# A four-layer vision hybrid on one core: where the mask's scatters stand, how late chunks are forced, and work moved between VectorE, GpSimd and ScalarE

## The chip, the cores and the metric

The kernel runs on one core of a Trainium2 chip, as one program. The metric is the device time of that program in microseconds. A profiled execution also gives the span, from the first recorded instruction to the last, and the TensorE clock that was granted, as a share of full speed. Engines are named TensorE (PE), VectorE (DVE), ScalarE (ACT), GpSimd (POOL) and SyncE (SP); PEld is TensorE's loading of weights.

## What is computed

The input `x` is 4 images of 32 x 32 positions with 256 channels, in float32. Four layers follow one another, image by image, with nothing shared between images except weights and one attention mask. The reference, cut to what matters here:

```python
# layer 0: conv, then a selective scan over the 1024 positions, 512 channels x 64 states
x = gelu(depthwise3x3(layernorm(src) @ w_in + b_in))
dt_raw, B, C = split(x @ w_x);  dt = softplus(dt_raw @ w_dt + dt_bias)
h = exp(dt*A)*h + (dt*x)*B;  y = sum_n h*C          # step by step over the positions
x = src + layernorm(y + x*D_skip) @ w_out + b_out
# layer 1: 1x1 conv, grouped 3x3 conv, 1x1 conv, residual
# layer 2: attention over 1024 positions, 8 heads, under a mask given by a list of edges
mask = zeros((N, N), bool).at[edge_index[0], edge_index[1]].set(True)
attn = softmax(where(mask, Q @ K.T / sqrt(32), -inf));  x = x + layernorm(ln(x) + (attn @ V) @ Wo + bo)
x = x + moe(ln(x))                                  # 8 experts of 256, best two of a position
# layer 3: a selective scan with 512 channels x 16 states, then 8 experts of 512, best two
x = x + scan3(ln(x));  out = x + moe(ln(x))
```

## The kernel before

**The stream of scans.** Each image has one scan of layer 0 and one of layer 3. A scan is cut into four chunks `d` of 128 channels, a chunk into units of 128 partitions x 1024 positions, where a partition is one channel with one state. A chunk of layer 0 has 64 units, a chunk of layer 3 has 16; with 4 images that is 1280 units in all. `SCANS` fixes their order: (layer, image) = (0,0), (0,1), (3,0), (0,2), (3,1), (0,3), (3,2), (3,3). `scans` (L340 to L477) issues a unit `k` as follows. `load` fetches the step sizes of unit k+4 by DMA into `dA` (5 buffers). `decay` makes exp(dt*A) of unit k+2 on ScalarE. `first` spreads the inputs of unit k+1 over the states on TensorE, into the PSUM tile `ps_rep` (2 buffers). VectorE multiplies `ps_rep` by the rows of B and runs the scan instruction into `h` (5 buffers); GpSimd multiplies `h` by the rows of C in place; and every second unit `pair` sums over the states of two units on TensorE into `ps_y`. So each unit takes two instructions of VectorE, one of ScalarE, one of GpSimd and some of TensorE, in a fixed order.

**The side work.** Everything else is written as generators that stop after every few instructions (`yield` with an estimated cost). `STAGES` lists them in order: `front(b)` of the four images (layer 0 up to the scan's inputs), `middle(b)` (`back0`, which ends layer 0 after its scan, layer 1, attention, the first mixture of experts, and `front3`, the inputs of layer 3's scan), and `last(b)` (the end of layer 3 and the second mixture of experts). A stage becomes available once the scan named beside it is done. `run` (L506) walks through the stream and, twice in each unit, lets the current stage go on by up to `TICKS` = 2 steps, as long as no engine's own clock of estimated work is ahead of VectorE's. The clocks are kept by the wrapper `Metered`, which adds an estimated cost for each instruction that goes through it (`Metered.COST`, L92 to L105; instructions issued through it carry L121 in the profile). `last(3)` is not in the list; `run` issues it when the stream is over.

**Forcing.** At unit k, `chunk(k + AHEAD)` with `AHEAD` = 12 (L461) fetches the inputs of a chunk if unit k+12 is a chunk's first. It calls `need(scan, d)` (L479), which lets the stages go on, with no unit in between, until the chunk's inputs (`parts`) are written. With every such step of a stage it also lets the work on the mask go on by `SORTS` = 2 steps, and at the end it sets all clocks to the furthest.

**The mask.** `mask_prepare` (L906) is one more generator, `mask_work`. It loads the list of edges, turns it into positions with transposes on TensorE, sorts each partition's positions in 68 steps on VectorE (L981 to L986), writes the sorted positions to `where`, and goes on into `scatter` (L992): 64 indirect DMAs, each of which writes one zero per partition to the mask in DRAM from GpSimd's queue, then four switches for longer lists that in this data leave their scatters out, and one DMA that casts the mask to bf16 (`maskT`). Outside `need`, `run` lets `mask_work` go on by one step in each unit.

**`steps`** (L538 to L598) ends `front` and `front3`. For each of 8 items of 128x512 it projects onto `ps_dt`, forms softplus from `sp_r`, `sp_e` and `sp_l` on ScalarE (relu, abs, exp, add 1, ln), VectorE (`add`, one instruction) and GpSimd (`add`, three instructions), and splits the product into three bf16 parts: a cast on ScalarE, the rest (`sp_x`) by a subtraction on VectorE, a second cast on ScalarE, and the lowest part on GpSimd. An item passes through `project`, `add`, `split`, `low` and `store` as through a pipe, one item apart.

**`attention`** (L1052) makes the scores `ps_sc`, their exponential `p`, and sums over keys with and without the values (`ps_at`), in `heads`. After every second pair of heads, four times an image, it takes the reciprocal of `sums` (128x512) on VectorE and multiplies `raw` by it on GpSimd (L1115 to L1120). `shift`, ahead of it, finds the number that is subtracted from the scores. The mixtures of experts work with `ps_h` (into an expert), `h_m` (gelu) and `ps_e` (out of it).

**`front`** (L634) loads its image `x` and the weights `w_in` first, then does the norm, the transposes, the projection and the 3x3 conv (`pad`, `ps_cv`), the projection to B, C and the step sizes, and `steps`.

Of the kernel before, what the change touches and what calls it, by code (L numbers as in the profile page):

```python
# [7 lines left out]
F32 = mybir.dt.float32  # L8
BF16 = mybir.dt.bfloat16
I32 = mybir.dt.int32  # L10
AF = mybir.ActivationFunctionType
ALU = mybir.AluOpType
# [4 lines left out]
P = 128  # L17
NB = 4
L = 1024
TB = L // P  # L20
C = 256
# [16 lines left out]
SAFE = 40.0  # L38
SORTS = 2
AHEAD = 12  # L40

# [82 lines left out]
class Hybrid:  # L126
    def __init__(self, ctx, tc, a, out):
        self.ctx, self.tc, self.nc, self.a = ctx, tc, tc.nc, a
        self.out = out.rearrange("b h w c -> (b h w) c")
        nc = self.nc  # L130
        self.const = const = ctx.enter_context(tc.tile_pool(name="const", bufs=1))
        self.dram = ctx.enter_context(tc.tile_pool(name="dram", bufs=1, space=DRAM))

        self.ident = const.tile([P, P], F32, name="ident")
        make_identity(nc, self.ident)
        self.identb = const.tile([P, P], BF16, name="identb")
        nc.vector.tensor_copy(self.identb, self.ident)

        order = const.tile([P, NEXP], I32, name="order")
        nc.gpsimd.iota(order, pattern=[[-1, NEXP]], base=NEXP, channel_multiplier=0)  # L140
        self.order = const.tile([P, NEXP], F32, name="orderf")
        nc.vector.tensor_copy(self.order, order)
        self.eps = {}
        for e in (1e-5, 1e-3):
            self.eps[e] = const.tile([P, 1], F32, name=f"eps{len(self.eps)}")
            nc.vector.memset(self.eps[e], e)

        self.mem = {}

# [190 lines left out]
    def scans(self, mp, psum):  # L340
# [9 lines left out]
        for scan in SCANS:  # L350
# [2 lines left out]
                (scan, d, c, i, j)  # L353
                for d in range(DC) for c in range(2) for i in range(32 // G) for j in range(2)
            ]
        chunks, rows = {}, {}
        state = {}
        y = None

        def chunk(k):  # L360

            if k >= len(units):
                return
            scan, d, c, i, j = units[k]
            if (c, i, j) != (0, 0, 0):
                return
            n = self.states[scan[0]]
            self.need(scan, d)
            if d == 0:
                bct = self.mem["bc", *scan]  # L370
                pair = []
                for t in range(2):
                    x = mp.tile([P, L], F32, tag=f"rows{t}", name=f"rows{t}", bufs=2)
                    for g in range(P // n):
                        nc.sync.dma_start(x[g * n : (g + 1) * n, :], bct[t * n : (t + 1) * n, :])
                    pair.append(x)
                rows[scan] = pair
            S = mp.tile([3 * 32, 4, L], BF16, tag="S", name="S", bufs=2)
            for s in range(3):
                nc.sync.dma_start(  # L380
                    S[32 * s : 32 * s + 32, :, :],
                    self.mem["parts", *scan, d][s].rearrange("(j p) t -> p j t", p=32),
                )
            chunks[scan, d] = S

        def load(k):
            if k >= len(units):
# [70 lines left out]
        decay(1)  # L458
        first(0)
        for k in range(len(units) + 4):  # L460
            chunk(k + AHEAD)  # L461
            load(k + 4)
            first(k + 1)
            decay(k + 2)
# [14 lines left out]
    def need(self, scan, d):  # L479

        late = False
        while ("parts", *scan, d) not in self.ready:
            if self.advance() is None:
                raise RuntimeError(f"{scan} waits for a stage that waits for it")
            late = True
            for _ in range(SORTS):
                next(self.mask_work, None)
        if late:

# [16 lines left out]
    def run(self):  # L506
# [4 lines left out]
        with tc.tile_pool(name="scan", bufs=1) as mp, tc.tile_pool(  # L511
            name="scps", bufs=1, space=PSUM
        ) as psum, tc.tile_pool(name="sdps", bufs=1, space=PSUM) as side, tc.manual_schedule():
            self.side_psum(side)
            self.mask_work = self.mask_prepare()
            clock = self.clock = dict.fromkeys(Metered.COST, 0.0)
            self.nc = Metered(nc, clock)
            for n, _ in enumerate(self.scans(mp, psum)):
# [19 lines left out]
    def steps(self, fp, key, w, src, chunks, bias, u):  # L538
# [33 lines left out]
        def split(item):  # L572
# [3 lines left out]
            X = fp.tile([P, 3, 512], BF16, tag="parts", name="parts", bufs=3)  # L576
            rest = tile2("x", 2)
            nc.scalar.copy(X[:, 0, :], x)
            nc.vector.tensor_tensor(rest, x, X[:, 0, :], ALU.subtract)
            nc.scalar.copy(X[:, 1, :], rest)  # L580
            got[item] = rest, X

# [51 lines left out]
    def front(self, b):  # L634
# [3 lines left out]
        with tc.tile_pool(name=f"f{b}", bufs=1, side="right") as op:  # L638
# [2 lines left out]
            nc.sync.dma_start(w_dt, self.a["L0_conv_w_dt"])  # L641
            u = op.tile([P, DC, L], F32, name="u0")
            with tc.tile_pool(name=f"fa{b}", bufs=1, side="right") as fp:
                x = fp.tile([P, TB, C], F32, name="x0")
                nc.sync.dma_start(x, self.image(self.a["x"].rearrange("b h w c -> (b h w) c"), b))
                w_in = self.weight(fp, "L0_conv_w_in", 2)
                pads = [fp.tile([P, 34, 34], F32, name=f"pad{i}") for i in range(2)]
                for i in range(2):
                    nc.gpsimd.memset(pads[i], 0.0)
# [256 lines left out]
    def mask_prepare(self):  # L906
# [16 lines left out]
        with tc.tile_pool(name="mprep", bufs=1) as mp:  # L923
# [5 lines left out]
            for a in range(2):  # L929
# [6 lines left out]
                    raw[:rest, full, :], edges[a, full * P * P :].rearrange("(r p) -> r p", p=P)  # L936
                )
                raws.append(raw)
            yield from [None] * 6
            for a, raw in enumerate(raws):  # L940
                rawf = mp.tile([P, full + 1, P], F32, tag="rawf", name="rawf", bufs=2)
                nc.vector.tensor_copy(rawf[:, :full, :], raw[:, :full, :])
# [44 lines left out]
            nc.vector.tensor_scalar(lin, order, 0.0, 2.0 * L * L, ALU.is_le, ALU.mult)  # L987
            nc.vector.scalar_tensor_tensor(lin, order, -1.0, lin, ALU.add, ALU.add)
            nc.vector.tensor_copy(self.where, lin)
        yield from self.scatter()  # L990

    def scatter(self):  # L992
# [35 lines left out]
    def prepare2(self, st, psum):  # L1028
# [17 lines left out]
        )  # L1046
        self.onesb = self.const.tile([P, P], BF16, name="onesb")
        nc.vector.memset(self.onesb, 1.0)
        self.ones = self.const.tile([P, 32], F32, name="ones32")
        nc.vector.memset(self.ones, 1.0)  # L1050

    def attention(self, b, tb):  # L1052
        nc, tc, vec = self.nc, self.tc, self.vec
        with tc.tile_pool(name=f"at{b}", bufs=1, side="right") as op:
# [48 lines left out]
            with tc.tile_pool(name=f"ac{b}", bufs=1, side="right") as fp:  # L1103
# [3 lines left out]
                for nh in range(2):  # L1107
# [3 lines left out]
                    for hp in range(4):  # L1111
                        yield from self.heads(fp, raw, sums, qT, kT, v, maskT, mT, nh, hp)
                        if hp % 2:
                            c = hp // 2
                            nc.vector.reciprocal(sums[:, c, :], sums[:, c, :])  # L1115
                            yield 2.0
                            nc.gpsimd.tensor_tensor(
                                raw[:, c, :], raw[:, c, :], sums[:, c, :], ALU.mult
                            )
# [614 lines left out]
```

## Time and profile before

The three timed runs of the kernel before took 6986.5, 7001.59 and 7013.21 us; the median is 7001.59 us. The profile is of one further execution:

| what | value |
|---|---|
| span of the profiled execution | 6998.6 us |
| its own time | 7000.6 us |
| instructions in the span | 66,229 |
| mean granted TensorE clock | 0.816 |
| GpSimd's `h` times rows, 1280 of them | 3029.4 us, 2369 ns each |
| VectorE's scans, 1280 | 2924.8 us, 2285 ns each |
| VectorE's `ps_rep` times rows, 1280 | 1553.1 us, 1213 ns each |
| ScalarE's exponentials of `dA`, 1280 | 1445.6 us, about 1146 ns each |
| ScalarE's table loads, 496 | 636.4 us, 1283 ns each |
| VectorE's two instructions of a unit together | 4477.9 us of its 5202.2 |
| data moved | 939 MB, 134 GB/s over the span |

The busy times of a page are sums over one execution, and an engine's share is of the whole span. Since the work comes in stretches with different limits (a head before the first scan, the stream, a stretch with no scan near the end, and a tail), such a share says little about any one of them. For that one reads the page's 40 slices, where VectorE falls to 2 tenths and 4 tenths from slice 33 on while TensorE goes on, and the timelines of single engines. "Idle before, releaser" is the idle time of that engine ahead of a group's instructions, and what ended most of it.

### The profile page before, as it was taken

How to read it: one execution, taken by the hardware profiler on the slowest of the kernel's cores; microseconds unless marked ns; L12 is line 12 of the kernel's file. 1: busy time of each engine (PE TensorE's matmuls, PEld its weight loads, DVE VectorE, ACT ScalarE, POOL GpSimd, SP SyncE). 2: the span in 40 equal slices, each digit the busy share in tenths (PEclk: the TensorE clock that was granted, in tenths of full speed). 3: DMA queues.
4: the chain of work that ended last, by engine and by line, in shares of the span. 5: the costliest groups of instructions: out<-in, count | busy, mean ns of one | idle time of the engine just before them, and what ended most of it. 6: DMA issues, size and time to landing. Idle time of an engine off the chain costs nothing. (4 is left out here: it accounts for less than half of the span.)

```text
span 6998.6 us, 66229 instructions
## 1 busy us (share of the span) xinstructions
PE 5362.1 (77%) x20433; PEld 2215.4 (32%) x20516; DVE 5202.2 (74%) x4476; ACT 3455.6 (49%) x4157; POOL 3646.1 (52%) x1801
## 2 busy tenths in 40 slices
PE   6267877578898557879779778898698677867979
PEld 2011211032242022224235332253254322523556
DVE  7379899887898986789889877898899830247511
ACT  2346666234577333447658434577386332244511
POOL 0667677565557755555756554556656530045300
PEclk8577867579898577889779778898699779877989
DMA  2356666654456565446656655456666630145421
GB/s 70 88 147 169 172 172 170 173 141 112 123 139 180 159 174 128 116 120 172 176 150 164 181 135 134 114 141 175 170 167 167 161 82 1 49 115 154 109 63 33
DMA packets 395050, 939.01 MB, mean 134 GB/s; under 512 B 83268, under 2 KB 165776, under 8 KB 393040
## 3 DMA queue, kind: packets, MB, share of 16 engines
q1 hardware_dynamic: 392512, 932.10, 49.6%
q8 instruction: 172, 2.82, 0.2%
q0 software_dynamic: 2128, 2.13, 0.2%
q14 instruction: 238, 1.95, 0.1%
HBM read 844.17 MB, written 93.95 MB: 134 GB/s over the span
## 5 line engine op out<-in xcount | busy, mean ns | idle before, releaser
L121 POOL TENSOR_TENSOR h<-h,rows 128x1024 f32<-128x1024 f32 x1280 | 3029.4, 2369 | 2048.6 <-DVE h L121 1661.0
L121 DVE TENSOR_TENSOR_SCAN h<-dA,ps_rep 128x1024 f32<-128x1024 f32 x1280 | 2924.8, 2285 | 214.1 <-issue 94.5
L121 DVE TENSOR_TENSOR ps_rep<-ps_rep,rows 128x1024 f32<-128x1024 f32 x1280 | 1553.1, 1213 | 330.9 <-PE ps_rep L121 310.6
L121 ACT ACTIVATE dA<-dA,A_L_conv_A_log 128x1024 f32<-128x1024 f32 x1024 | 1152.0, 1145 | 714.8 <-DMA dA<-dt 629.4
L121 PE MATMUL ps_rep<-S,spread_L_conv_A_log 96*128 96x512 bf16 x2048 | 759.1, 461 | 789.5 <-DVE h L121 730.6
L121 PE MATMUL ps_y<-h,collect_L_conv_A_log 128*32 128x512 f32 x4096 | 758.7, 754 | 87.9 <-POOL h L121 87.7
L121 ACT ACT_TABLE_LOAD x496 | 636.4, 1283 | 72.3 <-PE ps_h L121 50.3
L121 PEld LDWEIGHTS <-spread_L_conv_A_log 96*128 96x128 bf16 x2048 | 163.7, 103 | 1552.1 <-DVE h L121 1213.9
L121 PE MATMUL ps_h<-xTm,we 128*128 128x512 f32 x1280 | 605.7, 609 | 6.9 <-ACT h_m L121 5.8
L121 PE MATMUL ps_e<-we,h_m 128*128 128x256 f32 x2560 | 589.5, 382 | 8.3 <-ACT h_m L121 8.3
L121 ACT ACTIVATE p<-ps_sc 128x512 f32<-128x512 f32 x512 | 277.9, 594 | 588.7 <-PE ps_sc L121 431.7
L121 ACT ACTIVATE dA<-dA,A_L_attn_A_log 128x1024 f32<-128x1024 f32 x256 | 293.6, 1148 | 475.5 <-DMA dA<-dt 440.7
L121 PEld LDWEIGHTS ps_e<-we,h_m 128*128 128x128 f32 x2560 | 483.1, 190 | 138.8 <-issue 46.0
L121 PE MATMUL ps_at<-p,v 128*32 128x512 f32 x1024 | 361.6, 622 | 65.8 <-ACT p L121 58.0
L121 PE MATMUL ps_rep<-S,spread_L_attn_A_log 96*128 96x512 bf16 x512 | 191.7, 465 | 265.2 <-DVE h L121 219.5
L121 ACT ACTIVATE h_m<-ps_h,cols 128x512 f32<-128x512 f32 x320 | 216.7, 687 | 301.1 <-PE ps_h L121 298.3
L121 DVE SCALAR_TENSOR_TENSOR tb<-ps_e,cw,tb 128x256 f32<-128x256 f32 x448 | 192.7, 473 | 200.4 <-PE ps_e L121 200.4
L121 PEld LDWEIGHTS ps_h<-xTm,we 128*128 128x128 f32 x1280 | 242.3, 193 | 287.9 <-issue 239.7
L121 PE MATMUL ps_sc<-qT,kT 32*128 32x512 f32 x1024 | 299.5, 660 | 0.0
L121 PE MATMUL ps_at<-p,ones 128*32 128x512 f32 x1024 | 277.6, 622 | 0.0
L121 PE MATMUL ps_cv<-pad,diag 128*128 128x512 f32 x576 | 260.0, 593 | 0.0
L121 PEld LDWEIGHTS ps_y<-h,collect_L_conv_A_log 128*32 128x32 f32 x4096 | 99.2, 119 | 457.7 <-issue 226.4
(361 smaller groups left out, 5429.6 us busy)
## 6 DMA issues: line engine op xcount, KB each, us to landing
dA<-dt SPq DMA_DIRECT2D x2048, 256.0 KB
dA<-dt SPq DMA_DIRECT2D x2048, 64.0 KB
we<-in_L_ffn_W_dram SPq DMA_DIRECT2D x64, 512.0 KB
parts<-parts SPq DMA_DIRECT2D x64, 384.0 KB
S<-parts SPq DMA_DIRECT2D x96, 256.0 KB
dt<-sp_r SPq DMA_DIRECT2D x64, 256.0 KB
y<-yo SPq DMA_DIRECT2D x128, 128.0 KB
y_back<-y SPq DMA_DIRECT2D x64, 256.0 KB
```

Of the source, the lines that this page charges most:

```text
L121: return got(*args, **kw)
```

## The change

Nothing of what is computed changes; only where and when some of it is done.

- **Head.** The first image `x0` and the weights `w_in0` get tiles of their own for the whole program and are loaded ahead of everything else; `front(0)` reads that `x0`, and every `front` reads that `w_in0`. The wait between the loading of the edges and their conversion grows from 6 to 24 steps of `mask_work`.
- **Scatters.** When the sort is over, `mask_prepare` sets `self.sorted` and yields. From then on `need` no longer lets `mask_work` go on, so that the scatters come one a unit from `run`.
- **Late chunks.** `chunks_ahead` replaces `chunk(k + AHEAD)`. A chunk's first unit is put on a list at 12 units ahead. It is fetched at once if its inputs are there; otherwise it waits on the list until they are or until it is `LATEST` = 5 units ahead, and only then is it forced through `need`.
- **`rest`.** The subtraction that makes `sp_x` in `split` goes from VectorE to GpSimd, as a fifth instruction of GpSimd for each item.
- **Reciprocals.** VectorE's reciprocal of `sums` goes. In its place ScalarE takes ln and exp(-ln) into a new tile `inv`, with a table preload ahead; GpSimd multiplies `sums` and `raw` by it; ScalarE forms 2 minus the product, and GpSimd multiplies `raw` by that (one Newton step). A constant tile `two` is added, and the steps of the generator there have other costs.

```diff
--- before.py
+++ after.py
@@ -38,6 +38,7 @@
 SAFE = 40.0
 SORTS = 2
 AHEAD = 12
+LATEST = 5
 
 
 
@@ -144,6 +145,10 @@
         for e in (1e-5, 1e-3):
             self.eps[e] = const.tile([P, 1], F32, name=f"eps{len(self.eps)}")
             nc.vector.memset(self.eps[e], e)
+
+        self.x0 = const.tile([P, TB, C], F32, name="x0")
+        nc.sync.dma_start(self.x0, self.image(a["x"].rearrange("b h w c -> (b h w) c"), 0))
+        self.w_in0 = self.weight(const, "L0_conv_w_in", 2)
 
         self.mem = {}
 
@@ -353,7 +358,7 @@
                 (scan, d, c, i, j)
                 for d in range(DC) for c in range(2) for i in range(32 // G) for j in range(2)
             ]
-        chunks, rows = {}, {}
+        chunks, rows, waiting = {}, {}, []
         state = {}
         y = None
 
@@ -382,6 +387,16 @@
                     self.mem["parts", *scan, d][s].rearrange("(j p) t -> p j t", p=32),
                 )
             chunks[scan, d] = S
+
+        def chunks_ahead(k):
+
+            if k + AHEAD < len(units) and units[k + AHEAD][2:] == (0, 0, 0):
+                waiting.append(k + AHEAD)
+            while waiting:
+                scan, d = units[waiting[0]][:2]
+                if waiting[0] - k > LATEST and ("parts", *scan, d) not in self.ready:
+                    break
+                chunk(waiting.pop(0))
 
         def load(k):
             if k >= len(units):
@@ -458,7 +473,7 @@
         decay(1)
         first(0)
         for k in range(len(units) + 4):
-            chunk(k + AHEAD)
+            chunks_ahead(k)
             load(k + 4)
             first(k + 1)
             decay(k + 2)
@@ -483,7 +498,7 @@
             if self.advance() is None:
                 raise RuntimeError(f"{scan} waits for a stage that waits for it")
             late = True
-            for _ in range(SORTS):
+            for _ in range(0 if self.sorted else SORTS):
                 next(self.mask_work, None)
         if late:
 
@@ -512,7 +527,7 @@
             name="scps", bufs=1, space=PSUM
         ) as psum, tc.tile_pool(name="sdps", bufs=1, space=PSUM) as side, tc.manual_schedule():
             self.side_psum(side)
-            self.mask_work = self.mask_prepare()
+            self.mask_work, self.sorted = self.mask_prepare(), False
             clock = self.clock = dict.fromkeys(Metered.COST, 0.0)
             self.nc = Metered(nc, clock)
             for n, _ in enumerate(self.scans(mp, psum)):
@@ -576,7 +591,7 @@
             X = fp.tile([P, 3, 512], BF16, tag="parts", name="parts", bufs=3)
             rest = tile2("x", 2)
             nc.scalar.copy(X[:, 0, :], x)
-            nc.vector.tensor_tensor(rest, x, X[:, 0, :], ALU.subtract)
+            nc.gpsimd.tensor_tensor(rest, x, X[:, 0, :], ALU.subtract)
             nc.scalar.copy(X[:, 1, :], rest)
             got[item] = rest, X
 
@@ -641,9 +656,14 @@
             nc.sync.dma_start(w_dt, self.a["L0_conv_w_dt"])
             u = op.tile([P, DC, L], F32, name="u0")
             with tc.tile_pool(name=f"fa{b}", bufs=1, side="right") as fp:
-                x = fp.tile([P, TB, C], F32, name="x0")
-                nc.sync.dma_start(x, self.image(self.a["x"].rearrange("b h w c -> (b h w) c"), b))
-                w_in = self.weight(fp, "L0_conv_w_in", 2)
+                if b == 0:
+                    x = self.x0
+                else:
+                    x = fp.tile([P, TB, C], F32, name="x0")
+                    nc.sync.dma_start(
+                        x, self.image(self.a["x"].rearrange("b h w c -> (b h w) c"), b)
+                    )
+                w_in = self.w_in0
                 pads = [fp.tile([P, 34, 34], F32, name=f"pad{i}") for i in range(2)]
                 for i in range(2):
                     nc.gpsimd.memset(pads[i], 0.0)
@@ -936,7 +956,7 @@
                     raw[:rest, full, :], edges[a, full * P * P :].rearrange("(r p) -> r p", p=P)
                 )
                 raws.append(raw)
-            yield from [None] * 6
+            yield from [None] * 24
             for a, raw in enumerate(raws):
                 rawf = mp.tile([P, full + 1, P], F32, tag="rawf", name="rawf", bufs=2)
                 nc.vector.tensor_copy(rawf[:, :full, :], raw[:, :full, :])
@@ -987,6 +1007,8 @@
             nc.vector.tensor_scalar(lin, order, 0.0, 2.0 * L * L, ALU.is_le, ALU.mult)
             nc.vector.scalar_tensor_tensor(lin, order, -1.0, lin, ALU.add, ALU.add)
             nc.vector.tensor_copy(self.where, lin)
+        self.sorted = True
+        yield
         yield from self.scatter()
 
     def scatter(self):
@@ -1046,6 +1068,8 @@
         )
         self.onesb = self.const.tile([P, P], BF16, name="onesb")
         nc.vector.memset(self.onesb, 1.0)
+        self.two = self.const.tile([P, 1], F32, name="two")
+        nc.vector.memset(self.two, 2.0)
         self.ones = self.const.tile([P, 32], F32, name="ones32")
         nc.vector.memset(self.ones, 1.0)
 
@@ -1112,8 +1136,19 @@
                         yield from self.heads(fp, raw, sums, qT, kT, v, maskT, mT, nh, hp)
                         if hp % 2:
                             c = hp // 2
-                            nc.vector.reciprocal(sums[:, c, :], sums[:, c, :])
-                            yield 2.0
+
+                            r = fp.tile([P, 512], F32, tag="inv", name="inv", bufs=2)
+                            self.log_table()
+                            nc.scalar.activation(r, sums[:, c, :], AF.Ln)
+                            nc.scalar.activation(r, r, AF.Exp, scale=-1.0)
+                            yield 1.3
+                            nc.gpsimd.tensor_tensor(sums[:, c, :], sums[:, c, :], r, ALU.mult)
+                            nc.gpsimd.tensor_tensor(raw[:, c, :], raw[:, c, :], r, ALU.mult)
+                            yield 1.0
+                            nc.scalar.activation(
+                                sums[:, c, :], sums[:, c, :], AF.Identity, bias=self.two, scale=-1.0
+                            )
+                            yield 0.5
                             nc.gpsimd.tensor_tensor(
                                 raw[:, c, :], raw[:, c, :], sums[:, c, :], ALU.mult
                             )
```

## The prediction

> **What bounds the kernel now.** I read the page's engine lines first, then a table of busy time by stretch, then the timelines at the places where the stretches meet.
>
> ```profile
> PE 5362.1 (77%) x20433; PEld 2215.4 (32%) x20516; DVE 5202.2 (74%) x4476; ACT 3455.6 (49%) x4157; POOL 3646.1 (52%) x1801
> ```
>
> No engine is full over the span, so the limits are local. The stretches follow from VectorE's timeline, by counting its 1280 scans from 0 ("units"): the first starts at 279.9 us, unit 1203 at 5707.0, unit 1204 at 6224.1, and the last ends at 6582.5. In the table the columns after the stretch are its length and the busy us (count) of PE, PEld, DVE, ACT and POOL, then clock, DMA share and GB/s.
>
> ```profile
> 0.00:279.90 279.90, 122.55 (x286) 52.76 (x286) 146.20 (x333) 75.67 (x130) 68.67 (x70) 0.71 0.20 61
> 860.20:954.60 94.40, 57.28 (x144) 8.96 (x143) 84.47 (x57) 66.79 (x86) 85.71 (x50) 0.54 0.56 158
> 2310.60:2494.00 183.40, 100.99 (x310) 11.72 (x302) 173.83 (x102) 59.07 (x52) 120.01 (x52) 0.50 0.60 158
> 5709.30:6222.00 512.70, 424.65 (x1580) 182.47 (x1591) 75.50 (x181) 167.24 (x277) 45.74 (x36) 0.93 0.09 28
> 6222.00:6582.50 360.50, 261.81 (x965) 117.83 (x965) 292.16 (x235) 195.91 (x205) 207.07 (x101) 0.77 0.61 161
> 6582.50:6998.60 416.10, 371.42 (x1316) 251.60 (x1311) 58.47 (x150) 76.26 (x114) 17.07 (x13) 0.93 0.16 48
> ```
>
> Row 1 is the head, no scan. Row 3 is the bare stream, 51 units with no stage beside them: VectorE sets 3.60 us a unit. Row 2 is front(2)'s `steps`, 22 units at 4.29 us: VectorE and POOL are both near full. Row 4 is the hole: scan (3,3) waits for middle(3), PE works alone. Then scan (3,3) runs beside last(2), and the final row is the rest of last(2) and last(3), PE alone.
>
> In the head the timelines of VectorE and POOL show a queue, not work:
>
> ```profile
> 165.87 0.45 DVE L121 CAST where<-lin 128x544 int32<-128x544 f32 x1
> 175.08 0.69 DVE L121 SCALAR_TENSOR_TENSOR sp_e<-ps_dt,sp_e 128x512 f32<-128x512 f32 x1 [8.76 <-ACT sp_l L121]
> ```
> ```profile
> 234.25 0.97 POOL L121 DMA_INDIRECT mask_dram<-zero,where  x1 [1.43 <-DMA mask_dram<-zero,where]
> 236.65 0.97 POOL L121 DMA_INDIRECT mask_dram<-zero,where  x1 [1.43 <-DMA mask_dram<-zero,where]
> 237.64 1.27 POOL L121 TENSOR_TENSOR sp_l<-sp_l,sp_e 128x512 f32<-128x512 f32 x1
> ```
>
> `sp_e` was ready at 175.8, but 30 scatters at 2.40 us stand before `sp_l` on POOL until 237.6. In the stream a POOL burst reaches VectorE:
>
> ```profile
> 366.94 2.34 POOL L121 TENSOR_TENSOR h<-h,rows 128x1024 f32<-128x1024 f32 x1
> ```
> ```profile
> 372.27 1.23 DVE L121 TENSOR_TENSOR ps_rep<-ps_rep,rows 128x1024 f32<-128x1024 f32 x1 [6.82 <-PE ps_rep L121]
> ```
>
> Five instructions (361 to 367 us) hold this `h`, PE's `ps_y` behind it and the next `ps_rep`; VectorE stands 6.82 us.
>
> [...] here 128x512 takes 1.27 us on POOL and 0.68 on VectorE alone. [...] `sp_x` runs 0.682 to 2.294 us, median 1.513. [...] the trace's loads take 1283 ns, and one stands before each `steps` item. [...]
>
> **The change part by part.** The sum is made against the profiled execution: span 6998.6, its time 7000.6, 1.0 below the median of 7001.6. Positions are from the order of the changed program's instructions.
>
> *Head.* `x0` and `w_in` load first, the norm goes ahead of the sort, one scatter is left on POOL. PE's transposes still stand behind the edge transposes (about 58 us); the 97 us of conv and projection that before took 73.5 to 170 then end near 155. The sort now binds: 68 steps of 1.57 us (107) from about 57 end near 166. POOL starts `sp_l` at 168 instead of 237.6 (-70); from there to the first scan was 42.3, five rounds of about 8.5 us with two scatters each, and becomes about 40, as `rest` (1.29) takes their place. 279.9 becomes 208: -72. If the sort were hidden too, PE's chain would allow only 10 us more.
>
> *Scatters in the stream.* 63 of 64 now stand one behind each `h`: 2.37+1.03 = 3.40 us on POOL, under VectorE's 3.60, but nothing is left for `steps`: only two of its items fit in before unit 64, where 4 switches and the rest follow. Before, units 0 to 33 took 172.9 us. After, front(0) needs 74: 5 at 5, 59 at 3.75 (before, such units ran 3.6 with a few at 4 to 5), the last 10 with items, switches (27, as the gaps of 10.5 and 16.5 us at units 20 and 29) and the wait for front(1)'s x (15): 350. Less 41 bare units (148): +29. Without cover, at the 4.1 of the POOL-bound units, +50.
>
> *`rest` on POOL.* Off VectorE go 52 in the stream, about 1.5 us each. But POOL gets 5 instructions an item (6.35 us) at 3.60-2.37 = 1.23 us spare a unit, and the planner spaces an item 4.5 to 5 units instead of 3. So `steps` takes 35 to 37 units instead of 21 to 22. A unit then needs (4.75 x 2.37+6.35)/4.75 = 3.71 us of POOL and 3.74 of VectorE. The burst is longer than the slack before `h` is missed (about 5.5: three units less `h`, `ps_y`, `ps_rep`), and ScalarE's second cast, with the `dA` exponentials behind it, waits for POOL. I take 4.1 a unit (bounds 3.75 and 4.4). Before, 94.4+15 x 3.6 = 148; after 37 x 4.1 = 152; in the middles 96+50 = 146 against 35 x 4.1 = 144. Six such stages: +2 in all; bounds -75 and +65.
>
> *Reciprocals.* In heads stages a unit with one takes 9.7 us (units 584, 603, 618) instead of 3.6: 3.35 busy, 2.6 to 3.0 waiting for `sums`. Off the stream: 12 x 6.1 = 73. In their place stand a table load, Ln, Exp and a third pass on ScalarE (1.28+3 x 0.6) and two more POOL products (2.54); `dA` exponentials and the next `p` queue behind a pass that waits for POOL. No such wait is in the trace; bounds 0 and 6 us each, value 2.3. Net -45.
>
> *Late chunks.* LATEST acts at one place, (3,3): elsewhere the parts are ready 12 units ahead in both orders. But stretched stages push all later ones: middle(0) starts at unit 304 instead of 259, last(1) ends at 1173 instead of 1142, middle(3) starts at 1175 instead of 1155 and is forced at 1211 instead of 1204: 36 units of cover instead of 49. The stream gets 7 units (+25) and loses what stood in 1191 to 1204 (88 us, less 13 x 3.6: -41). Stream in all: 29+2-45+25-41 = -30.
>
> *Hole.* It takes 60 more `ps_sc` and 36 more `ps_at`: 9.5 rounds of 3.89 us (their period at 5714 to 5740): +37. The whole `shift` with its switch, +25 (estimate: 32 matmul pairs at 0.354 and four squares of 1.15, plus waits), and the mask's 2 MB load, +10. The reciprocal's chain was 3.35+1.27 and becomes 6.9 on three engines; with `p` behind it, +10 for four; POOL's `rest` in the last rounds, +6. +88.
>
> *After it.* 69 units instead of 76, but last(2) starts at 1229 instead of 1218: 18 units x 4.1, 30 as the 28 before (155.8+7), 21 x 4.25 = 328 against 358: -30. So 18 more `ps_h` (0.86) and 40 more `ps_e` (0.43) are left for the tail, by the chain's 6.87 us for 8 and 6.91 for 16: +33.
>
> Sum: -72-30+88-30+33 = -11. Span 6988, plus 2.0 around it, 6990.
>
> **Rivals.** *Even* (the forecast): the head's gain is paid out in the hole and the tail; 6990, own range 6967 to 7030. *POOL's bursts are hidden*: five `h` buffers absorb them, `steps` runs at 3.75 a unit (-75) and the reciprocal costs nothing in its new place (-28): 6890 to 6965, most likely 6930. For it: POOL is 52% busy, and before, bursts of four passed without a gap. Against: row 2 has POOL at 91%. *POOL becomes the bound* (slower): in `steps` each item's 6.35 us in one piece stops `h` and ScalarE's cast, so that VectorE stands 2 us or more an item beyond my value. At 4.4 a unit that is +65 and in units 0 to 74 +20: 7075. It decides from 4.25 a unit on; the gap of 6.82 us above is such a burst. *The change doesn't do what it says*: the later forcing covers nothing. By the order this is so already and is in the sum: 7 units are won, 20 lost before.
>
> **How the numbers follow.** Even 0.42, hidden 0.28, POOL bound 0.30. 0.5% (35 us) is about what a measurement of this kernel can tell from no change; the cases give faster 0.28, same 0.42, slower 0.30. The 8-in-10 range reaches into both neighbours: 6915 to 7075.
>
> **What would show it.** First scan near 208 us (200 to 220). Unit 74 some 350 us later. `steps` stages of 35 to 37 units at 4.1 us: under 3.85 speaks for hidden bursts, over 4.25 for POOL. No unit near 9.7 in the heads stages. A hole of about 605 us, PE full. A tail of about 449 after the last scan. A hole no longer than 517, or a first scan later than 240, would make the working wrong, not only a size.

## The result and the profile after

The changed kernel takes 7036.9 us (median of 8 runs, 7033.1 to 7040.3) against 7002.6 us for the kernel before (8 runs): a ratio of 1.0049, 95% interval 1.0038 to 1.0060. It is slower by half a per cent; 6990 was forecast, with a range of 6915 to 7075; the time lies inside it, on the wrong side of no change. The profiled execution has a span of 7035.0 us.

The engine lines of the changed kernel's page:

```profile
PE 5491.0 (78%) x20516; PEld 2227.5 (32%) x20516; DVE 5085.3 (72%) x4398; ACT 3466.5 (49%) x4196; POOL 3730.7 (53%) x1897
```

VectorE lost 117 us of work and GpSimd gained 85, as the change says. TensorE shows 129 us more with the same 20516 weight loads, which is the first sign of something else; "The clock" below comes back to it. The busy times by stretch, with the same columns as in the prediction; the rows are the head, the `steps` of `front(2)`, the hole, the units after it, and the tail:

```profile
0.00:207.90 207.90, 122.42 (x286) 54.33 (x286) 141.20 (x330) 71.37 (x126) 34.03 (x37) 0.81 0.25 82
977.00:1126.00 149.00, 89.62 (x245) 12.80 (x244) 132.60 (x86) 86.24 (x106) 136.67 (x80) 0.58 0.65 182
5646.00:6260.40 614.40, 491.01 (x1804) 207.92 (x1805) 63.47 (x183) 196.85 (x319) 63.83 (x51) 0.86 0.09 29
6260.40:6586.20 325.80, 225.20 (x806) 96.36 (x806) 260.31 (x208) 159.17 (x170) 193.92 (x97) 0.75 0.64 162
6586.20:7035.00 448.80, 403.73 (x1428) 269.96 (x1423) 62.72 (x160) 83.87 (x125) 17.06 (x13) 0.94 0.15 47
```

The head ends at 207.9 (forecast 208). `steps` has GpSimd 92% busy. The hole is 614.4 us long (605), the units after it take 325.8 (328) and the tail 448.8 (449). The stream from 207.9 to 5646.0 takes 5438 us where 5397 was forecast: the error sits there.

The head, in the timelines of VectorE and GpSimd:

```profile
169.69 0.44 DVE L122 CAST where<-lin 128x544 int32<-128x544 f32 x1
170.05 1.28 DVE L122 SCALAR_TENSOR_TENSOR sp_e<-ps_dt,sp_e 128x512 f32<-128x512 f32 x2
```
```profile
170.44 1.19 POOL L122 DMA_INDIRECT mask_dram<-zero,where  x1 [163.69 <-DVE where L122]
171.67 1.27 POOL L122 TENSOR_TENSOR sp_l<-sp_l,sp_e 128x512 f32<-128x512 f32 x1
```

`where` is done, one scatter goes, and `sp_l` follows at 171.7 instead of 237.6. In the stream the scatters stand between the products of GpSimd:

```profile
236.72 0.99 POOL L122 DMA_INDIRECT mask_dram<-zero,where  x1 [0.17 <-issue]
237.75 2.35 POOL L122 TENSOR_TENSOR h<-h,rows 128x1024 f32<-128x1024 f32 x1
240.41 1.00 POOL L122 DMA_INDIRECT mask_dram<-zero,where  x1 [0.31 <-DMA mask_dram<-zero,where]
```

The wait of 1.43 us that stood before each of them in the head is mostly gone here (0.17 us in the median of the stream's 63 scatters): it passes while the product runs (2.35 us).

Now the second reciprocal of image 0 (the chain of ScalarE, GpSimd, TensorE and VectorE, one view each, in the changed kernel):

```profile
1776.42 1.28 ACT L246 ACT_TABLE_LOAD   x1
1777.71 0.63 ACT L122 ACTIVATE inv<-sums 128x512 f32<-128x512 f32 x1
1778.37 0.63 ACT L122 ACTIVATE inv<-inv 128x512 f32<-128x512 f32 x1
```
```profile
1779.08 1.27 POOL L122 TENSOR_TENSOR sums<-sums,inv 128x512 f32<-128x512 f32 x1 [4.05 <-ACT inv L122]
1780.30 1.27 POOL L122 TENSOR_TENSOR raw<-raw,inv 128x512 f32<-128x512 f32 x1
1781.53 2.35 POOL L122 TENSOR_TENSOR h<-h,rows 128x1024 f32<-128x1024 f32 x1
1783.83 1.26 POOL L122 TENSOR_TENSOR raw<-raw,sums 128x512 f32<-128x512 f32 x1
```
```profile
1785.15 2.93 PE L122 MATMUL ps_wo<-w_L_attn_Wo,raw 128*128 128x256 f32 x6 [7.81 <-POOL raw L122]
```
```profile
1788.11 0.69 DVE L122 TENSOR_TENSOR y_at<-ps_wo,xa 128x512 f32<-128x512 f32 x1 [9.72 <-PE ps_wo L122]
```

and the same place in the kernel before, VectorE and TensorE:

```profile
1707.34 3.35 DVE L121 RECIPROCAL sums<-sums 128x512 f32<-128x512 f32 x1 [2.56 <-ACT sums L121]
1710.62 2.23 DVE L121 TENSOR_TENSOR_SCAN h<-dA,ps_rep 128x1024 f32<-128x1024 f32 x1
1715.06 0.69 DVE L121 TENSOR_TENSOR y_at<-ps_wo,xa 128x512 f32<-128x512 f32 x1 [2.22 <-PE ps_wo L121]
```
```profile
1712.10 6.33 PE L121 MATMUL ps_wo<-w_L_attn_Wo,raw 128*128 128x256 f32 x14 [4.78 <-POOL raw L121]
```

Read from the moment when `sums` is there (1707.3 before, 1776.4 after) to `y_at`: 7.7 us before, 11.7 after. GpSimd's four instructions are a queue in which an `h` of the stream (2.35) stands inside the chain. `ps_wo` waits 7.81 us for `raw` instead of 4.78, and TensorE makes its next `ps_rep` only behind it, at 1787.9. VectorE, which no longer has a reciprocal to do, waits at its own next instruction, `y_at`, which stands ahead of the next `ps_rep` product. Over the whole program, who waited before `ps_wo` and `y_at` (us, times), first before, then after:

```profile
  POOL raw L121: 76.3, 16
  PE ps_wo L121: 31.2, 16
```
```profile
  PE ps_wo L122: 384.9, 16
  POOL raw L122: 124.3, 16
```

The numbers for `raw` count each wait of TensorE twice, for the matmul and for its weight load. The numbers for `ps_wo` mix the stream with the hole, where VectorE has little else to do: 312.6 of the 384.9 us stand there. In the stream alone, at 12 of the 16 reciprocals, VectorE before waited 37.0 us for `sums`, worked 40.2 us on the reciprocals and waited 19.9 us at `y_at`, together 97 us; after, it waits 72.3 us at `y_at`. That alone would be a gain. The loss stands one instruction further on: in the three stages of `heads` beside the stream, VectorE's waits for the next `ps_rep` grew from 135 to 206 us.

Only every second reciprocal has a `ps_wo` behind it. Behind the first of each pair stand the next scores, and there the chain reaches TensorE through `p`. Three of ScalarE's instructions and one of VectorE's at the first reciprocal of image 0, in the changed kernel:

```profile
1699.14 1.28 ACT L246 ACT_TABLE_LOAD   x1
1703.10 0.72 ACT L122 ACTIVATE sums<-sums,two 128x512 f32<-128x512 f32 x1 [0.34 <-POOL sums L122]
1703.85 1.09 ACT L122 ACTIVATE p<-ps_sc 128x512 f32<-128x512 f32 x2
```
```profile
1717.28 1.23 DVE L122 TENSOR_TENSOR ps_rep<-ps_rep,rows 128x1024 f32<-128x1024 f32 x1 [10.09 <-PE ps_rep L122]
```

The scores are there at 1701.2, but `p` starts behind the table load, Ln, Exp, an exponential of `dA` and the third pass. TensorE waits for `p`, and VectorE then 10.09 us for its next `ps_rep`. The reciprocal's work went away from VectorE, and its waits became longer.

### The profile page after: what moved, and what is told of

The parts are those of the page before. It is cut to its first block, busy times and chain, and to the rows that moved or that the text cites. A ratio compares the mean times of both kernels' runs of the same rounds, so it can differ in the third digit from the quotient of the medians.

```text
span 7035.0 us, 66406 instructions
## 1 busy us (share of the span) xinstructions
PE 5491.0 (78%) x20516; PEld 2227.5 (32%) x20516; DVE 5085.3 (72%) x4398; ACT 3466.5 (49%) x4196; POOL 3730.7 (53%) x1897
## 3 DMA queue, kind: packets, MB, share of 16 engines
q8 instruction: 173, 2.83, 0.2%
## 5 line engine op out<-in xcount | busy, mean ns | idle before, releaser
L122 PE MATMUL ps_y<-h,collect_L_conv_A_log 128*32 128x512 f32 x4096 | 836.1, 749 | 134.3 <-POOL h L122 133.7
L122 PE MATMUL ps_at<-p,v 128*32 128x512 f32 x1024 | 397.1, 647 | 84.6 <-ACT p L122 72.4
L122 PEld LDWEIGHTS ps_h<-xTm,we 128*128 128x128 f32 x1280 | 243.1, 193 | 284.1 <-issue 235.4
L122 PEld LDWEIGHTS ps_y<-h,collect_L_conv_A_log 128*32 128x32 f32 x4096 | 116.5, 119 | 553.2 <-POOL h L122 320.8
L122 DVE TENSOR_TENSOR y_at<-ps_wo,xa 128x512 f32<-128x512 f32 x16 | 11.1, 692 | 384.9 <-PE ps_wo L122 384.9
```

The lines of the kernel that those rows point to most:

```text
L122: return got(*args, **kw)
```

## The experiments

Theory A: the new reciprocal is the larger loss, because its chain over three engines stands in TensorE's queue. Theory B: the rest on GpSimd costs little by itself, but the stages that it stretches take cover from the hole. Their rivals: GpSimd's load is the loss; the scatters in the stream give back what the head gains; late forcing brings or costs something of its own. Each run had the kernel before beside it, so the ratios to it are compared; 0.1% is 7 us.

| kernel | median us | ratio to before, 95% | head | stream | hole | units after | tail |
|---|---|---|---|---|---|---|---|
| before | 7002.6 | 1 | 279.9 | 5427 | 517 | 358 | 416 |
| changed | 7036.9 | 1.0049 (1.0038 to 1.0060) | 207.9 | 5438 | 614 | 326 | 449 |
| e1_recip_vector | 6947.9 | 0.9916 (0.9901 to 0.9930) | 207.5 | 5400 | 550 | 326 | 452 |
| e2_rest_vector | 7016.5 | 1.0019 (1.0012 to 1.0025) | 204.5 | 5538 | 513 | 329 | 433 |
| e3_both_vector | 6925.4 | 0.9883 (0.9868 to 0.9899) | 207.3 | 5473 | 486 | 328 | 433 |
| e4_latest12 | 7018.0 | 1.0019 (1.0012 to 1.0027) | 205.1 | 5413 | 607 | 359 | 433 |
| e6_no_newton | 6959.2 | 0.9948 (0.9934 to 0.9962) | 204.5 | 5480 | 505 | 332 | 433 |
| e7_newton_vector | 7029.2 | 1.0040 (1.0026 to 1.0053) | 204.5 | 5561 | 502 | 331 | 430 |
| e8_rest_unmetered | 6907.3 | 0.9861 (0.9846 to 0.9876) | 210.5 | 5447 | 488 | 325 | 444 |
| e9_both_latest12 | 6926.6 | 0.9890 (0.9875 to 0.9905) | 205.1 | 5430 | 518 | 358 | 420 |
| e10_both_scatter_head | 6961.8 | 0.9954 (0.9939 to 0.9969) | 235.4 | 5462 | 485 | 328 | 433 |
| e11_both_late_loads | 6904.8 | 0.9873 (0.9858 to 0.9888) | 209.8 | 5440 | 488 | 332 | 433 |
| e12_raw_vector | 6892.8 | 0.9847 (0.9834 to 0.9861) | 205.7 | 5439 | 484 | 319 | 443 |
| e13_best | 6897.1 | 0.9861 (0.9845 to 0.9878) | 207.7 | 5432 | 490 | 324 | 441 |

The stretches are of the profiled executions; the hole starts behind unit 1210, in e4, e9 and before behind 1203. A profiled execution can lie up to 18 us off its kernel's median: those of e1 (6937) and e10 (6944) are faster than their medians, that of e8 (6916) is slower.

**One part undone: the reciprocal, the rest, both.**

```diff
 # e1, e3 (the removed statements are shortened)
-r = fp.tile(...); self.log_table(); Ln; Exp(-1); sums *= r; raw *= r; sums = 2 - sums
+nc.vector.reciprocal(sums[:, c, :], sums[:, c, :])
+yield 2.0
 # e2, e3
-nc.gpsimd.tensor_tensor(rest, x, X[:, 0, :], ALU.subtract)
+nc.vector.tensor_tensor(rest, x, X[:, 0, :], ALU.subtract)
```

Expected of e1:

> The changed kernel with the reciprocal of the sums back on VectorE, all else as changed. Theory (the chain of the new reciprocal stands in TensorE's queue ahead of the next ps_rep and costs about 8 us more than VectorE's reciprocal at each of 12 places in the stream, and more in the hole): about 6960 us (6945 to 6980), 75 us below the changed kernel, with the heads stages at 325 to 340 us for 67 units as before the change. Rival (the rest on GpSimd is what makes the changed kernel slower, the reciprocal is neutral): 7025 to 7045.

Expected of e2:

> The changed kernel with the rest back on VectorE, the new reciprocal kept. Theory (reciprocal chain is the larger loss; the rest on GpSimd gains some 57 us in the stream and loses about 100 in the hole and the tail through 20 units less of cover): about 6980 us (6960 to 7000). Rival (the rest on GpSimd is the main loss): below 6950.

Expected of e3:

> The changed kernel with both the rest and the reciprocal back on VectorE: only the head, the scatters in the stream and the late chunks are left of the change. Theory: first scan at about 208 us instead of 280, units 0 to 74 as in the changed kernel, stages after that where they stood before the change, forced hole at unit 1210: about 6915 us (6900 to 6940). Rival (the scatters in the stream give back what the head gains): 6985 to 7005.

Undoing the reciprocal is worth 1.33% with the rest on GpSimd (changed to e1) and 1.36% with the rest on VectorE (e2 to e3): some 94 us, independent of the other part. Undoing the rest is worth 0.30% (changed to e2) and 0.33% (e1 to e3), some 22 us. So the reciprocal is the larger loss, as theory A has it, and e3 shows that the gain of the head stays when the scatters stand in the stream: -1.2%. e2 missed its forecast of 6980 by 36 us: the reciprocal costs 65 us in the stream and 27 in the hole (5538 against 5473, 513 against 486), more than was allowed for. The hole of e2 also holds two rounds of scores more than that of e3, some 8 of the 27 us.

Where in the stream: the three `heads` stages take 356.8, 368.0 and 365.2 us for 70 units in e2, and 324.1, 340.0 and 339.4 for 67 in e3. Less 9 bare units of 3.60 that is 54 us for 12 places, 4.5 each. Both kinds of place lose about the same: over eleven units, from two before the reciprocal on, the time beyond 3.60 us a unit has a median of 9.4 us at the six first places and 21.4 at the six second ones in e3, and of 14.0 and 26.1 in e2.

In the hole of e1 TensorE has 459.7 us of work against 491.0, and 90 us of gaps against 123:

```profile
5607.00:6157.00 550.00, 459.69 (x1696) 191.43 (x1711) 75.26 (x180) 176.05 (x294) 50.27 (x40) 0.90 0.08 27
```

The 31 us less of work are there in the main because three shorter `heads` stages let `middle(3)` begin at unit 1169 instead of 1175; the rest is the chain, four times, and a clock of 0.90 instead of 0.86.

**Which part of the reciprocal.** Both start from e2 (rest on VectorE). e6 leaves out the Newton step, so the reciprocal is only what ln and exp give:

```diff
 # e6
-nc.gpsimd.tensor_tensor(sums[:, c, :], sums[:, c, :], r, ALU.mult)
-nc.gpsimd.tensor_tensor(raw[:, c, :], raw[:, c, :], r, ALU.mult)
-nc.scalar.activation(sums[:, c, :], sums[:, c, :], AF.Identity, bias=self.two, scale=-1.0)
-nc.gpsimd.tensor_tensor(raw[:, c, :], raw[:, c, :], sums[:, c, :], ALU.mult)
+nc.gpsimd.tensor_tensor(raw[:, c, :], raw[:, c, :], r, ALU.mult)
 # e7
-nc.scalar.activation(sums[:, c, :], sums[:, c, :], AF.Identity, bias=self.two, scale=-1.0)
+nc.vector.tensor_scalar(sums[:, c, :], sums[:, c, :], -1.0, 2.0, ALU.mult, ALU.add)
```

Expected of e6:

> The kernel with the rest on VectorE and the new reciprocal, without its Newton step (two products of GpSimd and one pass of ScalarE less at each place, so the reciprocal is only as exact as ln and exp). The chain from sums to raw is then a table load, two passes and one product, 3.8 us by its rows, against 4.6 with VectorE's reciprocal. Theory (the length of the chain in TensorE's queue is the cost): most of the 91 us between this kernel with the Newton step (7016) and VectorE's reciprocal (6925) goes: 6940 (6925 to 6955). Rival (ScalarE's table load, Ln and Exp ahead of the exponentials are the cost): 6980 to 7005.

Expected of e7:

> The same with the Newton step kept, but its pass 2 - s on VectorE instead of ScalarE. Theory (length of the chain): little changes, and VectorE now waits for GpSimd's product: 7015 (7000 to 7035). Rival (the exponentials p and dA that queue on ScalarE behind the pass that waits for GpSimd are the cost): 6950 to 6985.

The waits before `ps_wo` and `y_at` in e6, then in e7:

```profile
  PE ps_wo L122: 278.3, 16
  POOL raw L122: 62.5, 16
```
```profile
  POOL raw L122: 154.6, 16
  PE ps_wo L122: 61.6, 16
```

TensorE has two waits to compare. In the three stages of `heads` beside the stream, each wait counted once (us):

| kernel | ratio to before | TensorE's wait for `raw` | for `p` |
|---|---|---|---|
| e3, VectorE's reciprocal | 0.9883 | 27 | 22 |
| e6, no Newton step | 0.9948 | 22 | 46 |
| e2, with Newton step | 1.0019 | 47 | 39 |
| e7, its pass on VectorE | 1.0040 | 62 | 23 |

Of the 1.36% between e3 and e2, 0.71% goes with the Newton step, and with it the longer wait for `raw`. e6 came out at 6959, between the forecast and the rival's range: 0.65%, 45 us, remain (28 us in the profiled executions, 20 of them in the hole), although TensorE waits less for `raw` than with VectorE's reciprocal. What remains longer is its wait for `p`, 46 us against 22, and what e6 still has on ScalarE ahead of `p` is a table load, Ln and Exp. No run takes these alone away, so the waits support this cause but do not isolate it. In e7 the wait for `p` is back at 23 us without the pass on ScalarE; but the pass now waits for GpSimd's product in VectorE's queue (59 us in these stages), `raw` comes later, and the whole is slower. So theory A, the length of the chain to `raw`, accounts for about half of the loss.

**The clock.** After a gap of TensorE its granted clock was also lower. Around the first reciprocal of image 0 (1701 us) the changed kernel's stretches read (the number after POOL's busy time is the granted clock), and TensorE's timeline ahead of them has the gap:

```profile
1704.50 1.55 PE L122 MATMUL ps_at<-p,v 128*32 128x512 f32 x2 [2.83 <-ACT p L122]
```

```profile
1702.00:1708.00 6.00, 3.50 (x12) 1.01 (x14) 5.00 (x3) 3.60 (x5) 6.00 (x5) 0.69 0.53 148
1708.00:1716.00 8.00, 7.74 (x24) 1.46 (x21) 0.00 (x0) 1.09 (x3) 4.44 (x2) 0.50 0.28 66
```

TensorE waits 2.83 us for `p`, then is busy for 7.74 of 8.00 us at a clock of 0.50, while VectorE does nothing (0.00). The kernel before has 1.00 at the same place (1628 to 1646 us). In the changed kernel's trace the granted clock is 0.5 or 1.0, 142 stretches of each, and each but the last, which runs past the end of the span, lasts 3.41 us or a multiple of it. In the 3.41 us from 1700.9 us on, which hold most of the gap, TensorE was 23% busy at a clock of 1.0; the next 13.65 us, four times 3.41, ran at 0.5, with TensorE over 90% busy in each of the four. Between 1000 and 3000 us of the changed kernel, 123 of the 124 pieces of 3.41 us that follow one with TensorE (matmuls and weight loads) less than half busy are at 0.5, and 323 of the 353 that follow one over 90% busy are at 1.0. From the first to the last scores of `heads` the mean clock went from 0.94 to 0.90 in image 0 (1564.7 to 1863.4 us before, 1620.1 to 1945.9 after) and from 0.93 to 0.90 in image 2 (4193.1 to 4500.5, 4189.3 to 4519.6); in image 1 it was 0.90 and 0.91 (2723.5 to 3037.6, 2679.6 to 3002.5). Over the whole span TensorE was busy at half clock for 1460 us instead of 1361, which is 99 of the 129 us by which its busy time grew, although the mean granted clock of the span, 0.822 against 0.816, did not fall. What the clock alone costs no run isolates.

**The rest on GpSimd, without the planner's count.** From e1, the instruction is issued past the wrapper that counts:

```diff
-nc.gpsimd.tensor_tensor(rest, x, X[:, 0, :], ALU.subtract)
+nc.what.gpsimd.tensor_tensor(rest, x, X[:, 0, :], ALU.subtract)
```

Expected of e8:

> The kernel with VectorE's reciprocal and the rest on GpSimd, where the planner is not told of the rest's cost on GpSimd, so that the steps stages take about 27 units instead of 37 and the middle of the last image starts at unit 1155 instead of 1169. Theory (the rest on GpSimd costs through the cover that the stretched stages take from the hole): below the 6948 us of the kernel in which it is counted: 6922 (6905 to 6938). Rival (GpSimd's bursts themselves cost): 6945 to 6975.

The same instructions on the same engine, 0.55% faster than e1. In the middles `steps` takes 27 units instead of about 37, at 4.4 us (118 us against 107 for 22 in the kernel before, so about 7 us less with 3.60 for each of the 5), and the hole is shorter:

```profile
5657.80:6145.50 487.70, 404.47 (x1450) 178.26 (x1461) 72.30 (x179) 156.42 (x258) 49.15 (x40) 0.90 0.09 29
```

55 us less of TensorE's work stands in it than in e1's, because `middle(3)` begins at unit 1155 again. The stream is 48 us longer, the hole 62 and the tail 8 shorter; the profiled executions differ by 22 us in all, the medians by 0.55%, some 38. Theory B holds: the price of the rest on GpSimd is the cover that the planner gives away for it, not GpSimd's bursts. Against the rest on VectorE (e3) it is 0.22% ahead, with intervals that overlap.

**LATEST.** `LATEST = 12` on the changed kernel (e4) and on e3 (e9):

Expected of e4:

> The changed kernel with LATEST = 12, so that late chunks are forced 12 units ahead as before the change. Theory: it acts in one place, scan (3,3); forced at unit 1203 instead of 1210, so 7 units' worth of stage work goes from the stream into the hole, about +15 us: 7052 (7040 to 7065). Rival (the later forcing brings nothing, or harms): 7020 to 7038.

Expected of e9:

> The kernel with the rest and the reciprocal on VectorE (6925 us) and LATEST = 12. Theory after the run with LATEST = 12 on the changed kernel: later forcing takes 7 units from the last stages beside scan (3,3), about 16 us of tail, and pays only if these units cover heavy TensorE work before the hole. Here heads runs in them (16 of 128 ps_sc pairs more), so both nearly balance: 6930 (6918 to 6945). Rival (later forcing never pays): 6900 to 6915.

e4 went against me: forcing 12 units ahead is 0.30% faster than 5, and its 7018.0 us lie even below the rival's range. The tail tells why: 433 us against 449. `last(2)` begins 18 units after the forced hole in both, so seven units later forcing are seven units less for its experts beside scan (3,3). And before the hole these seven units cover almost nothing (3.7 us each, the hole is 614 against 607 us). In e9, where the scores of `heads` run there, the hole grows from 486 to 518 when they are taken away, the tail shrinks by 13, and the times agree within their intervals.

**Scatters and early loads.** From e3, e10 lets the forcing go on with the scatters, and e11 loads `x` and `w_in` in each `front` as before:

```diff
 # e10
-for _ in range(0 if self.sorted else SORTS):
+for _ in range(SORTS):
 # e11
-self.x0 = const.tile([P, TB, C], F32, name="x0")
-nc.sync.dma_start(self.x0, self.image(a["x"].rearrange("b h w c -> (b h w) c"), 0))
-self.w_in0 = self.weight(const, "L0_conv_w_in", 2)
...
-w_in = self.w_in0
+w_in = self.weight(fp, "L0_conv_w_in", 2)
```

Expected of e10:

> The kernel with the rest and the reciprocal on VectorE (6925 us), where the forcing before the first scan goes on with the scatters after the sort as before the change, so that about 18 of the 63 go back into the head. Theory (a scatter in the head costs its 2.40 us in front of sp_l, and nothing measurable in the stream): first scan near 250 us, 6965 us in all (6950 to 6980). Rival (in the stream a scatter costs about the same): 6918 to 6935.

Expected of e11:

> The same kernel (6925 us), where x and w_in are loaded inside each front as before the change, after the loads of the setup. Theory (with the scatters gone from the head, the sort and the front's chain end within 10 us of each other, so that the early loads are worth little): first scan near 217 us, 6935 us in all (6925 to 6945). Rival (the early loads are the main gain of the head): above 6960.

In e10, 11 scatters stand before the first `sp_l` and 19 before the first scan:

```profile
192.50 0.97 POOL L122 DMA_INDIRECT mask_dram<-zero,where  x1 [1.46 <-DMA mask_dram<-zero,where]
193.48 1.29 POOL L122 TENSOR_TENSOR sp_l<-sp_l,sp_e 128x512 f32<-128x512 f32 x1
```

`sp_l` starts 22.0 us later (11 x 2.4 is 26), the first scan 28 us later, at 235.4 (near 250 was expected); the stream gets back 11 in the profiled executions. By the runs it is 0.71% slower, more than the trace explains; its five runs spread over 35 us, and the profiled one is the fastest of them. Either way, a scatter in the head costs more than in the stream. e11 has its first scan at 209.8 us instead of 207.3: the early loads bring the norm from 40.8 to 6.4 us, and nothing follows, because `where`, the sort's result, is written from 172.1 on instead of 169.5. Its median lies 20 us under the range that was expected, but its ratio and e3's overlap.

**Further.** e12 takes e8 and puts the last product on VectorE (`nc.vector.tensor_tensor(raw, raw, sums)`); e13 adds the late loads to e12.

Expected of e12:

> The kernel with the uncounted rest on GpSimd and VectorE's reciprocal (6907 us), where the product of raw with the reciprocal also goes to VectorE. Theory (what counts at these 16 places is how long ps_wo stands in TensorE's queue for raw): the chain is 0.6 us shorter and does not stand behind a product of GpSimd: 6895 (6885 to 6905). Rival (VectorE's own time is the limit there, 0.68 us more of it at each place): 6907 to 6920.

Expected of e13:

> What the runs so far point to, put together: the scatters in the stream, LATEST = 5, the rest on GpSimd but not counted by the planner, the reciprocal and the product of raw on VectorE, and x and w_in loaded inside each front. If the 20 us that the late loads gained without a change in the head are real, 6872 us (6865 to 6885); if they belonged to that chip and run, 6890 (6882 to 6900).

e12 is at 0.9847, 0.14% under e8, the size that was expected, but the intervals overlap. e13 is at 0.9861: the 20 us by which e11's median lay under e3's don't come again. e12 has the lowest ratio here, 1.5% under the kernel before (0.9834 to 0.9861) and 2.0% under the changed one; e8 and e13 cannot be told from it.

## Why the prediction was wrong

The sum of the prediction beside the profiled executions (us, after less before):

| step | forecast | measured |
|---|---|---|
| head | -72 | -72 |
| units 0 to 74 | +29 | +4 |
| `steps`, six stages | +2 | -56 |
| reciprocals in the stream | -45 | +51 |
| late chunks and the shifted start of `middle(3)` | -16 | -26 |
| stream, not priced | 0 | +38 |
| hole | +88 | +97 |
| units after it | -30 | -33 |
| tail | +33 | +33 |
| sum | -11 | +36 |

Inside the stream the measured column is the time of the units of a stage less 3.60 us for each, after less before; for the units 0 to 74 it is 324.4 - 172.9 - 41 x 3.6, and the late chunks have 7 units (25 us) added. That the sum missed by only 47 us is in part luck: the reciprocals in the stream came out 96 us worse than forecast, and `steps`, the units 0 to 74 and the late chunks together 93 us better.

- **The step that failed is "Reciprocals".** It took the 9.7 us of a unit with one as something that belongs to VectorE's instruction: 3.35 of work and 2.6 to 3.0 of wait, "Off the stream: 12 x 6.1 = 73", and put 2.3 us each against it, with 6 as the upper bound. The wait belonged to TensorE's queue, which stands for `raw` at `ps_wo` behind the second reciprocal of a pair and for `p` behind the first; VectorE's next instructions, `y_at` and the `ps_rep` product, inherit it. By e2 and e3 the new form costs 4.5 us a place more than VectorE's reciprocal, where 3.8 less was forecast. In the forecast's own terms, what was put in place of the 6.1 us costs 6.1 + 4.5 = 10.6 us and not 2.3, which is outside its bounds. The sign that the prediction had asked for, no unit near 9.7 us, failed at once: these units take 8.7 to 17.6 us. The queue of `p` was named and priced inside the 2.3; missing were `raw`'s reader on TensorE and the `h` that stands on GpSimd inside the chain.
- **Hole.** Right in size, not in its parts. By an estimate from the traces, with 3.89 us a round, the rounds of scores are +35 (37 forecast), `shift` and the mask ahead of them +30 (35), and what comes after the last `ps_wo` +1 (6). The four reciprocals are then about +32 and not +10: from the first score to the last `ps_wo` the hole takes 62 us beyond its 64 rounds (256 weight loads of `ps_sc`, four a round), at a mean clock of 0.88, and took 30 beyond its 55, at 0.96.
- **Head.** Right in size and in cause: e10 and e11 show that the scatters were the queue and that the sort then binds.
- **Units 0 to 74** were over-priced by 25 us. Up to unit 64 they took 252 us (246 forecast); the last ten, with items of `steps`, the switches and the wait for the next image, took 72 instead of 104. The gaps of before were too dear a price for these.
- **`steps`.** 37 or 38 units at 3.9 to 4.1 us in the fronts (37 at 4.1 forecast) and 36 or 37 at 4.0 to 4.2 in the middles: the after side was nearly right. The before side was under-counted: the window of 94.4 us holds the starts of 20 scans and not of 22, about 4.6 us a unit and not 4.29, and it leaves out the stage's first and last items, with which the stage takes 25 units and 116.1 us in `front(1)`. So the rest on GpSimd gains 9 us a stage in the stream, and the 14 units by which its stretched stages move `middle(3)` (1155 to 1169 in e1) are what the hole pays for it.
- **Late chunks.** The shifts were right to the unit, and so were the tail and the units after the hole. "7 units are won" was wrong: e4 shows that they are lost here.
- **Not priced**, +38: among it the experts of the three middles beside the stream (+11) and the part of `front3` ahead of `steps` (+13); the rest lies in the other stages and between them. None of it was followed further, and its cause stays open.
- **Rivals.** "POOL becomes the bound" put the loss into `steps` at 4.4 us a unit; it is about 4.0 with GpSimd 92% busy (149.0 us for 37 units), so the side came out as that rival said and for another reason. "Bursts are hidden" was nearer for `steps` and wrong on the reciprocal, which did not cost nothing.

## What to carry to other kernels

A wait that stands before an instruction is not removed with the instruction (here VectorE's waits for `ps_rep` went from 135 to 206 us): follow the data on to its next reader on every engine that works through a queue, and ask which instruction of the engine that was freed will wait for the same thing. Here one operation of 3.35 us on one engine beat a chain of shorter ones on three by 4.5 us a place, where each hand-over stood in another engine's queue. Where a planner counts costs, moving work to an engine also moves when later stages start (`middle(3)` from unit 1155 to 1169 in e1), and that is paid in the stretch that has no cover (550 us in e1, 488 in e8).

## What was not expected of the hardware

A gap of TensorE came with a second loss: after a wait of 2.83 us, in 3.41 us that were 23% busy, its granted clock was 0.5 for 13.65 us, and the two `ps_sc` matmuls with `maskT` took 1.03 us (from 1709.28 us on) instead of 0.60 (1700.63). In the head of the kernel before, an indirect DMA of GpSimd that follows another took 0.97 us and waited 1.43 us; in the changed kernel's stream, with a product of 2.35 us between two of them, the wait was 0.17 us in the median.
